# Checks split and moved ahead of the experts, filler matmuls behind the attention, output loads merged and placed ahead of the stores

## The chip, the core and the metric

The kernel runs on one core of one Trainium2 chip. The metric is the device time of one execution in microseconds, the median of three. A core has five engines with a queue of instructions each: TensorE (PE) for matrix products, VectorE (DVE), ScalarE (ACT), GpSimd (POOL) and SyncE (SP), which here issues most of the DMA. An engine works through its queue in order; a wait at its head holds up everything behind it. In the profile PEld is TensorE's loading of weights.

## The reference

Two layers over a tensor of 4 images, 128 channels and 64 x 64 positions (4096 tokens for each image), all in float32:

```python
def reference(x, ...):
    # layer 0
    x = x + _L0_conv_ref(_gn(x), ...)
    # layer 1
    t = _to_tokens(x)
    t = t + _L1_attn_ref(_ln_t(t), L1_attn_Wq, L1_attn_Wk, L1_attn_Wv)
    t = t + _L1_ffn_ref(_ln_t(t), L1_ffn_gate_w, L1_ffn_gate_b, L1_ffn_weight1, L1_ffn_weight2)
    return _from_tokens(t, x)
```

Layer 0 is an attention over the positions whose queries, keys and values are 1x1 convolutions with a PReLU. Layer 1 is an attention over the tokens and then a layer of 64 experts. Each expert picks 8 tokens of an image:

```python
    logits = jnp.einsum('bsd,ed->bse', x, gate_w) + gate_b
    probs = jax.nn.softmax(logits, axis=1)
    vals, idx = jax.lax.top_k(probs.transpose(0, 2, 1), K)
    ...
    pooled = jnp.einsum('bked,bke->bed', gathered, topv)
    h = jax.nn.gelu(jnp.einsum('ebd,edh->ebh', h, weight1), approximate=False)
    out = jnp.einsum('ebh,eho->ebo', h, weight2)
    ...
    outputs = outputs.at[jnp.arange(Bn)[:, None], flat_idx].add(weighted)
```

The chosen tokens are pooled with their weights, the pooled row goes through the expert's two matrices (128 to 512 to 128), and the result is added back to the chosen tokens.

## The kernel before

The softmaxes are computed without subtracting a maximum. The kernel therefore keeps the sums and their inverses (`all_sum`, `all_inv` for layer 0, `top_sum`, `top_inv` for layer 1), and `watch` turns them into one count of good partitions. When the count is below 128, a second, general program runs instead; the data at hand never need it.

**Stages.** `stage(b, layer, ...)` runs the attention of one image and layer: eight blocks of 512 queries, for each of them eight groups of four key tiles (`attention`). Each group is products into `ps`, an exponential on ACT, and the products with the values one group later (`products`). Work for other images is dealt out beside the groups. The last stage is `stage(3, 1, ...)`, image 3, layer 1, with `first_weights` beside it, which loads expert weights ahead of time.

**Behind the attention.** After the last stage the kernel finishes the last block of the last image, with nothing beside it. `finish_attn` combines the parts of the result on VectorE (`u`), multiplies by the value matrix on TensorE (`pv`, in two halves, L647), divides by the sum (`xT`, L655), normalizes the rows (`norm_tokens`, whose power runs on GpSimd, L181), transposes them (`x_c` L356 for the residual, `l` L678 for the gate), and forms the gate's logits (`pg`, L710). `last_route` then finds the eight best tokens for each expert among those of the last block and an earlier list: a chain of some twenty small VectorE instructions from `r_top` (L883) to `zl` (L916). Transposes (`pzT`, L923) and products (`pool`, L928 and L932) end in `pooledT`.

**Experts.** 64 experts run in 16 groups of four. Each group has 2 MB of packed weights, which come by two loads of 1 MB on SP into one of nine places (`places_of`); groups 0 to 8 go into the places 0 to 8, group g + 9 into the place that group g has left. Place 8, `late_place`, is 4096 columns wide and lies where the buffers of the routing lay; it can be loaded only when these have been read. The loop is a pipeline: `first_product(g)` (`ph` L1127 and the copy `hp` L1132), `hidden(g - 1)` (transposes `pht` L1137, bias `hT` L1141, Gelu L1145), `second_product(g - 2)` (`po` L1157). `ph`, `pot` and the product of `watch` share two PSUM buffers (`ms_tile`), so a new one waits until the one before the last has been copied out. `po` uses the two larger buffers (`sc_tile`) that the attention's `ps` used.

After group `half_g + 3`, which is 11, the loop does two things outside its own work: `next(scores)` replaces the eight best values in a row of 4096 on VectorE (L768), and `watch` reduces the four tensors, compares them and counts with a product of one column (L1703 to L1721).

**Output.** For each pair of images, `px` (L1217) spreads the experts' results over the tokens, VectorE adds them to the residual in place (L1224), and ACT issues the stores (L1227). The residual `x2` is loaded into places that the experts have left. Its loads stand on SP behind the weights and behind `first_pair`, the routing weights of images 0 and 1.

**What sets the order.** Instructions are recorded in the order of the program, and a scheduler then orders them for each engine; `keep_in_program_order` fixes an instruction against its neighbours, and `no_sync_barrier` keeps instructions on their side of it. DMAs take one of eight semaphores in turn, from SP and ACT alike, in the scheduled order; a DMA waits until the last user of its semaphore has landed.

Of the kernel before, what the change touches and what calls it, by code (L numbers as in the profile page):

```python
# [9 lines left out]
F32 = mybir.dt.float32  # L10
AF = mybir.ActivationFunctionType
ALU = mybir.AluOpType
AX = mybir.AxisListType
# [13 lines left out]
def tile_unshifted(  # L27
# [58 lines left out]

    x2 = [dram_tile([P, S], f"x2_{b}") for b in range(B)]
    x2_block = [[dram_tile([P, BLK], f"xb_{b}_{n}") for n in range(NB)] for b in range(B)]  # L90

    t1 = [[dram_tile([P, BLK], f"t1_{b}_{n}") for n in range(NB)] for b in range(B)]
# [522 lines left out]
    def finish_attn(b, n):  # L615
# [27 lines left out]
        for k, (s0, ns) in enumerate(((2, 2), (0, 2)) if final else ((0, 3), (3, 1))):  # L643
            pv = ms_tile(f"pv{nm}_{k}")[:, : ns * (C + 1)].rearrange("p (s c) -> p s c", c=C + 1)
            for s in range(ns):
                for h in range(2):
                    nc.tensor.matmul(  # L647
                        pv[bass.ts(h, HC), s, :],
                        lhsT=u[:, (s0 + s) * P + h * HC : (s0 + s) * P + (h + 1) * HC], rhs=wvd,
                        start=True, stop=True,  # L650
                    )
            i = slice((b * NB + n) * SUB + s0, (b * NB + n) * SUB + s0 + ns)
            nc.vector.reciprocal(top_inv[:, i], pv[:, :, C])
            for s in range(ns):
                nc.vector.scalar_tensor_tensor(  # L655
                    xT[:, s0 + s, :], in0=pv[:, s, :C],
                    scalar=top_inv[:, i.start + s : i.start + s + 1], in1=xq[:, s0 + s, :],
                    op0=ALU.mult, op1=ALU.add,
                )
            nc.vector.tensor_copy(top_sum[:, i], pv[:, :, C])  # L660
        yield
        tb = pools["blk"].tile([P, SUB, C], F32, tag="tb", name=f"tb{nm}")
        tg = block_tile("c1", f"tg{nm}")
        if direct:
            norm_tokens(xT, tb, f"l2_{b}_{n}")
            if not final:
                store_tokens(b, n, tb)
            xp = block_tile("xp", f"xp{nm}")
            to_channels(xT, xp, f"x2_{b}_{n}")
            nc.scalar.dma_start(out=x2[b][:, bass.ts(n, BLK)], in_=xp)  # L670
            yield
            if final:

                last_tokens.append(tb)
                for h, copy in enumerate((nc.scalar.copy, nc.vector.tensor_copy)):
                    pt = ms_tile(f"l2_{b}_{n}_{h}")[:, :HB]
                    for s in range(SUB // 2):
                        nc.tensor.transpose(  # L678
                            pt[:, bass.ts(s, P)], tb[:, h * SUB // 2 + s, :], ident
                        )  # L680
                    copy(tg[:, bass.ts(h, HB)], pt)
            else:
                to_channels(tb, tg, f"l2_{b}_{n}")
        else:
            turn_to_channels(
                xT.rearrange("p s c -> p (s c)"), block_tile("xp", f"xt{nm}"),
                x2_block[b][n],
            )
            yield
            norm_tokens(xT, tb, f"l2_{b}_{n}")  # L690
            store_tokens(b, n, tb)
            turn_to_channels(
                tb.rearrange("p s c -> p (s c)"), block_tile("c0", f"tt{nm}"), t2[b][n]
            )
            yield
            yield
            nc.sync.dma_start(out=tg, in_=t2[b][n])
            nc.sync.dma_start(out=x2[b][:, bass.ts(n, BLK)], in_=x2_block[b][n])
            yield
# [264 lines left out]
            yield  # L964


    def run(gen):
        for _ in gen:
            pass
# [74 lines left out]

    def first_weights():

        w1b = block_tile("xq", "w1b", 4)[:E, :]
        nc.sync.dma_start(out=w1b, in_=a["weight1"][:, D1 - 1, :])
        yield from idle(2)
        new_place(6, seq, "k")  # L1050
        new_place(2, extra, "w")
        for g in (6, 2):
            for h in range(2):
                load(g, g, h)
        yield from idle(2)
        pw = ms_tile("pw")
        for c in range(NHC):
            nc.tensor.transpose(
                pw[:, bass.ts(c, E)], w1b.rearrange("e (p c) -> e c p", c=NHC)[:, c, :],
                ident[:E, :E],  # L1060
            )
        nc.scalar.copy(w1bT.rearrange("p c e -> p (c e)"), pw[:, : NHC * E])
        yield from idle(2)
        new_place(7, seq, "v")
        for h in range(2):
            load(7, 7, h)
        yield

    def last_weights(n, g):
# [4 lines left out]
        if n == NB - 1:  # L1074
# [17 lines left out]
    stage(3, 1, chain(done_after(route(2)), first_weights()), None,  # L1092
          ahead=mix_values(3), pace=(2, 1), hook=last_weights)
    products()


    ends["att"].close()
# [7 lines left out]
    for g in range(3, 6):  # L1105
        new_place(g, ring, "w")
        for h in range(2):
            load(g, g, h)
    last_top = last_route(B - 1, pooledT)
    ends["blk"].close()  # L1110
    late = ctx.enter_context(tc.tile_pool(name="late", bufs=1, side="right", reuse_waits="tile"))
    late_place = late.tile([P, S], F32, tag="z", name="late_place")
    place(8, late_place)
    scores = last_scores(B - 1, *last_top)

    for h in range(2):
        load(8, 8, h)
# [58 lines left out]
    for g in range(E // EG + 2):  # L1176
        if g < E // EG:
            first_product(g)
        if 0 <= g - 1 < E // EG:
            hidden(g - 1)  # L1180
        if 0 <= g - 2:
            second_product(g - 2)

        for half, now in ((0, g), (1, g - 2)):
            if 0 <= now and now + 9 < E // EG:
                load(now + 9, now, half)
        if g == half_g + 3:
            next(scores)
            watch(ms_tile("watch")[0:1, 0:1])
    next(scores)  # L1190


# [5 lines left out]
    for i in range(B // 2):  # L1198
        for q in range(2):
            ys.append(places_of[2 * i + q])  # L1200
            for h in range(2):
                tc.keep_in_program_order(
                    nc.sync.dma_start(out=ys[-1][:, h, :], in_=x2[2 * i + h][:, bass.ts(q, HS)])
                )
    for i in range(B // 2):
        pe = ms_tile(f"poe{i}")
        nc.tensor.transpose(
# [471 lines left out]
@with_exitstack  # L1679
def tile_conv_attn_hybrid(ctx: ExitStack, tc: tile.TileContext, a: dict, out: bass.AP):  # L1680

    nc = tc.nc
    guard = ctx.enter_context(tc.tile_pool(name="guard", bufs=1))
    all_sum = guard.tile([P, BLK], F32, tag="all_sum", name="all_sum")
    all_inv = guard.tile([P, P], F32, tag="all_inv", name="all_inv")  # L1690
    nc.gpsimd.memset(all_sum, 0.0)
    nc.gpsimd.memset(all_inv, 0.0)
    top_sum = guard.tile([P, P], F32, tag="top_sum", name="top_sum")
    top_inv = guard.tile([P, P], F32, tag="top_inv", name="top_inv")
    nc.gpsimd.memset(top_sum, 0.0)
    nc.gpsimd.memset(top_inv, 0.0)
    count = guard.tile([1, 1], mybir.dt.int32, tag="count", name="count")

    def watch(pc):
        ok = guard.tile([P, 4], F32, tag="ok", name="ok")  # L1700

        later = tc.keep_in_program_order
        later(nc.vector.tensor_reduce(ok[:, 0:1], all_sum, axis=AX.X, op=ALU.max))  # L1703
        later(nc.vector.tensor_reduce(ok[:, 1:2], all_inv, axis=AX.X, op=ALU.max))
        nc.vector.tensor_scalar(ok[:, 0:1], ok[:, 0:1], SAFE_SUM, None, op0=ALU.is_le)
        nc.vector.tensor_scalar(ok[:, 1:2], ok[:, 1:2], SAFE_INV, None, op0=ALU.is_le)
        later(nc.vector.tensor_reduce(ok[:, 2:3], top_sum, axis=AX.X, op=ALU.max))
        later(nc.vector.tensor_reduce(ok[:, 3:4], top_inv, axis=AX.X, op=ALU.max))
        nc.vector.tensor_mul(ok[:, 2:3], ok[:, 2:3], ok[:, 3:4])
        nc.vector.tensor_scalar(ok[:, 2:3], ok[:, 2:3], SAFE_RATIO, None, op0=ALU.is_le)  # L1710

        later(nc.vector.tensor_reduce(ok[:, 3:4], top_inv, axis=AX.X, op=ALU.add))
        nc.vector.tensor_scalar(ok[:, 3:4], ok[:, 3:4], SAFE_INV, None, op0=ALU.is_le)
        both = guard.tile([P, 1], F32, tag="both", name="both")
        nc.vector.tensor_mul(both, ok[:, 0:1], ok[:, 1:2])
        nc.vector.tensor_mul(both, both, ok[:, 2:3])
        nc.vector.tensor_mul(both, both, ok[:, 3:4])
        ones = guard.tile([P, 1], F32, tag="ones_g", name="ones_g")
        nc.gpsimd.memset(ones, 1.0)
        nc.tensor.matmul(pc, lhsT=both, rhs=ones, start=True, stop=True)  # L1720
        nc.vector.tensor_copy(count, pc)  # L1721

    tile_unshifted(tc, a, out, all_sum, all_inv, top_sum, top_inv, watch)
    good = nc.values_load(count[0:1, 0:1], min_val=0, max_val=P)
    with tc.If(good < P):
        tile_general(tc, a, out)
# [40 lines left out]
```

## Time and profile before

| | us |
|---|---|
| median of three runs | 3296.14 (3294.93 to 3297.43) |
| the profiled execution | 3298.76 |
| its span, first to last instruction | 3297.0 |
| TensorE busy in the span | 3227.0 (98%) |
| VectorE busy | 2123.0 (64%) |
| end of the last attention product | 3179.2 |
| first product of the experts | 3202.5 |
| last product of the experts ends | 3257.2 |
| first add of the output | 3264.4 |
| last add of the output ends | 3286.8 |

The times on the lower half of the table are positions in the span. A row of the profile's timeline gives the start, the duration, the engine, the line, the operation, the tiles written and read, and how many instructions were merged; a float32 product appears as two records. The chain of waits gives start, duration and the instruction that was last on the way to the end. In the table by windows the columns are the length of the window, the busy time of each engine with its number of instructions, the granted clock of TensorE as a share of full speed, the share of the 16 DMA engines that was busy, and the bytes moved in GB/s. A wait line names the waiting instruction, what it waited for, the time in total, the number of waits and the longest.

### The profile page before, as it was taken

Reading aid. Unit: us, or ns where it says so; the run is one execution under the profiler, and the core shown is the slowest. Engines: PE = TensorE matmul, PEld = TensorE weight load, DVE = VectorE, ACT = ScalarE, POOL = GpSimd, SP = SyncE. Lnnn points to the kernel's source line nnn. Section 1 sums busy time; section 2 is a strip of 40 time slices with the busy share of each in tenths; the row PEclk is TensorE's granted clock in tenths of the full one; section 3 lists DMA queues with packets and bytes.
Section 4 is the critical chain, followed back from the end, with each engine's and each line's share of the span. In section 5 each row is a group of like instructions: output and inputs, shape, how many; then the busy total and the mean of one; then the engine's idle time right before and its main releaser. Section 6 shows DMA issues by size and latency. Waiting matters only on the chain.

```text
span 3297.0 us, 49453 instructions
## 1 busy us (share of the span) xinstructions
PE 3227.0 (98%) x19764; PEld 1602.7 (49%) x19764; DVE 2123.0 (64%) x4192; ACT 1253.4 (38%) x1432; POOL 424.4 (13%) x414
## 2 busy tenths in 40 slices
PE   8999999999999999999999999999999999999986
PEld 4444444445555644444555554444444455454443
DVE  6665567556665667756675657765776566666566
ACT  2333334433333335333433335333333333343432
POOL 0111112310000004241000002242100002010011
PEclk9999999999999999999999999999999999999988
DMA  3221244223323222311120111321231010131059
GB/s 88 52 53 28 56 113 122 74 82 80 90 73 85 55 55 54 70 31 36 39 53 23 39 26 39 91 64 26 45 75 39 20 40 20 33 108 39 17 203 373
DMA packets 364753, 223.31 MB, mean 68 GB/s; under 512 B 273632, under 2 KB 298720, under 8 KB 359136
## 3 DMA queue, kind: packets, MB, share of 16 engines
q1 hardware_dynamic: 359056, 208.54, 23.6%
q10 hardware_dynamic: 4944, 10.46, 0.8%
q8 instruction: 157, 2.57, 0.3%
q0 software_dynamic: 512, 1.05, 0.1%
q14 instruction: 84, 0.69, 0.1%
HBM read 159.75 MB, written 97.19 MB: 78 GB/s over the span
## 4 chain that ended last, share of the span: by engine, by line
PE 96%; DVE 2%; DMA 1%; issue 0%; POOL 0%; ACT 0%; SPq 0%; ACTq 0%; DVEq 0%; POOLq 0%
PE ps L542 40%; PE av L476 27%; PE av L504 23%; PE pe L272 1%; PE pa L291 1%; PE pq L445 1%; PE pv L647 1%; PE ph L1127 1%; PE pg L710 0%; PE po L1157 0%; PE pd L590 0%; PE pht L1137 0%; DMA w<-x 0%; DVE tt L490 0%; DMA first_x<-in_x_dram 0%
## 5 line engine op out<-in xcount | busy, mean ns | idle before, releaser
L551 ACT ACTIVATE pt<-ps 128x1024 f32<-128x1024 f32 x1024 | 1021.7, 1024 | 1520.0 <-PE ps L542 1452.7
L542 PE MATMUL ps<-q,t 128*64 128x512 f32 x4096 | 929.3, 593 | 0.0
L476 PE MATMUL av<-pt,asm 64*128 64x512 f32 x4096 | 922.2, 589 | 0.9 <-ACT sw L630 0.9
L566 DVE TENSOR_TENSOR sacc<-sacc,pt 128x1024 f32<-128x1024 f32 x448 | 586.0, 1308 | 290.6 <-ACT pt L551 265.8
L504 PE MATMUL av<-pt,tt 128*64 128x256 f32 x3072 | 637.6, 379 | 0.0
L476 PEld LDWEIGHTS av<-pt,asm 64*128 64x128 f32 x4096 | 395.8, 187 | 485.5 <-issue 470.1
L490 DVE TENSOR_TENSOR tt<-pt 128x512 f32<-128x512 f32 x512 | 356.7, 697 | 372.6 <-ACT pt L551 355.9
L542 PEld LDWEIGHTS ps<-q,t 128*64 128x64 f32 x4096 | 315.8, 137 | 469.4 <-issue 442.1
L504 PE MATMUL av<-tt,mixed 128*64 128x256 f32 x2048 | 526.9, 380 | 5.4 <-DVE tt L490 5.4
L542 PE MATMUL ps<-e,e 64*128 64x512 f32 x2048 | 491.5, 597 | 2.1 <-DMA e<-ye 2.1
L504 PEld LDWEIGHTS av<-pt,tt 128*64 128x64 f32 x3072 | 359.9, 137 | 261.8 <-issue 137.9
L504 PE MATMUL av<-pt,mixed 128*64 128x256 f32 x1024 | 305.5, 380 | 0.0
L504 PE MATMUL av<-tt,tt 128*64 128x256 f32 x1024 | 305.2, 380 | 0.0
L542 PEld LDWEIGHTS ps<-e,e 64*128 64x128 f32 x2048 | 193.0, 187 | 230.5 <-issue 226.6
L504 PEld LDWEIGHTS av<-tt,mixed 128*64 128x64 f32 x2048 | 280.8, 137 | 8.6 <-DVE tt L490 6.3
L181 POOL TENSOR_TENSOR l_y<-l_v,mhalf 128x4 f32<-128x4 f32 x64 | 64.9, 1014 | 1586.8 <-DVE l_v L180 1586.5
L492 DVE TENSOR_TENSOR tt<-pt 128x256 f32<-128x256 f32 x512 | 220.5, 431 | 16.5
L491 DVE TENSOR_TENSOR pt<-tt,pt 128x256 f32<-128x256 f32 x512 | 218.6, 427 | 16.2
L504 PEld LDWEIGHTS av<-pt,mixed 128*64 128x64 f32 x1024 | 140.3, 137 | 61.3 <-DVE pt L491 0.3
L504 PEld LDWEIGHTS av<-tt,tt 128*64 128x64 f32 x1024 | 140.5, 137 | 1.9 <-DVE tt L492 0.7
L585 POOL TENSOR_TENSOR all_sum<-all_sum,c 128x512 f32<-128x512 f32 x32 | 44.0, 1375 | 522.2 <-DVE c L584 522.2
L182 DVE TENSOR_TENSOR l_z<-l_y 128x4 f32<-128x4 f32 x64 | 11.7, 183 | 97.0 <-POOL l_y L181 97.0
(248 smaller groups left out, 1779.3 us busy)
## 6 DMA issues: line engine op xcount, KB each, us to landing
wp<-in_weight_dram SPq DMA_DIRECT2D x128, 256.0 KB
w<-wp SPq DMA_DIRECT2D x22, 1024.0 KB
xq<-in_x_dram SPq DMA_DIRECT2D x32, 256.0 KB
rb<-inv SPq DMA_DIRECT2D x32, 256.0 KB
xT<-xt SPq DMA_DIRECT2D x128, 64.0 KB
ak<-xT SPq DMA_DIRECT2D x32, 256.0 KB
t<-kt SPq DMA_DIRECT2D x128, 64.0 KB
t<-t SPq DMA_DIRECT2D x32, 256.0 KB
```

The costliest lines, as they stand in the source:

```text
L181: nc.gpsimd.tensor_tensor(y[:, :k], v[:, :k], mhalf[:, :k], op=ALU.pow)
L272: nc.tensor.matmul(pe[part, :], lhsT=w12[:, part], rhs=xn, start=True, stop=True)
L291: nc.tensor.matmul(pa[part, bass.ts(s, P)], lhsT=xn[:, bass.ts(s, P)][:, part], rhs=wa, start=True, stop=True,)
L476: nc.tensor.matmul(avs[b, 0, n][:, r, :], lhsT=values[b, 0][rows, j, :], rhs=pt[rows, h, :], start=(j == 0), stop=(j == NJ - 1),)
L490: nc.vector.tensor_sub(tt[:, 0:2, :], p4[:, :, 1, :], p4[:, 0, :, :])
L491: nc.vector.tensor_add(p4[:, 0, 1, :], tt[:, 1, :], p4[:, 0, 0, :])
L492: nc.vector.tensor_sub(tt[:, 2, :], p4[:, 1, 0, :], p4[:, 0, 1, :])
L504: nc.tensor.matmul(av[bass.ts(half, HC), bank, slot, :], lhsT=lhsT, rhs=rhs, start=first, stop=final, skip_group_check=True,)
L542: nc.tensor.matmul(ps[part, h, :], lhsT=key[:, part], rhs=q[rows, :], start=True, stop=True,)
L551: nc.scalar.activation(pt, ps, AF.Exp, scale=scale)
L566: nc.vector.tensor_add(sums[b, n], sums[b, n], pt)
L585: nc.gpsimd.tensor_add(all_sum, all_sum, c1)
```

## The change

Three things are changed.

1. `watch` is split. The part for layer 0 (five VectorE instructions) runs at the start of `first_weights`, in the last stage. The part for layer 1 (eight VectorE instructions) stands behind `last_route`, ahead of the experts. In the loop only the counting product and its copy are left, and these and `next(scores)` come after group `half_g + 2`, which is 10.
2. `keep_busy` puts products of the identity with itself, which nothing reads, into TensorE's queue: 11 behind the last attention product, 2 and 3 behind the two halves of `pv`, 9 behind the transposes `x_c`, and 24 ahead of the transposes `pzT`. They write to an `sc_tile`.
3. `x2` is kept by pairs of images, so that one DMA of 2 MB loads half the columns of both; four loads take the place of eight. A barrier for the scheduler stands between these loads and the output's products, adds and stores.

```diff
-    x2 = [dram_tile([P, S], f"x2_{b}") for b in range(B)]
+    x2_pair = [dram_tile([2, P, S], f"x2_{i}") for i in range(B // 2)]
+    x2 = [x2_pair[b // 2][b % 2] for b in range(B)]
...
             nc.vector.tensor_copy(top_sum[:, i], pv[:, :, C])
+            if final:
+                keep_busy(FILL[1 + k], f"busy_b{k}")
...
             nc.scalar.dma_start(out=x2[b][:, bass.ts(n, BLK)], in_=xp)
+            if final:
+                keep_busy(FILL[3], "busy_c")
...
+    FILL = (11, 2, 3, 9, 24)
+
+    def keep_busy(k, name):
+
+        t = sc_tile(name)
+        for i in range(k):
+            tc.keep_in_program_order(
+                nc.tensor.matmul(t[:, i % 2, :P], lhsT=ident, rhs=ident, start=True, stop=True)
+            )
...
     def first_weights():
 
+        watch(0)
...
     products()
+    keep_busy(FILL[0], "busy_a")
...
+    keep_busy(FILL[4], "busy_d")
     last_top = last_route(B - 1, pooledT)
...
     scores = last_scores(B - 1, *last_top)
+    watch(1)
...
-        if g == half_g + 3:
+        if g == half_g + 2:
             next(scores)
-            watch(ms_tile("watch")[0:1, 0:1])
+            watch(1, ms_tile("watch")[0:1, 0:1])
...
             ys.append(places_of[2 * i + q])
-            for h in range(2):
-                tc.keep_in_program_order(
-                    nc.sync.dma_start(out=ys[-1][:, h, :], in_=x2[2 * i + h][:, bass.ts(q, HS)])
+            tc.keep_in_program_order(
+                nc.sync.dma_start(
+                    out=ys[-1],
+                    in_=x2_pair[i].rearrange("h c t -> c h t")[:, :, bass.ts(q, HS)],
                 )
+            )
+
+    tc.no_sync_barrier()
```

The new `watch` in full; the old one did all of it in one call, with the result of each part multiplied into `both`:

```python
    def watch(layer, pc=None):
        later = tc.keep_in_program_order
        if layer == 0:
            later(nc.vector.tensor_reduce(ok[:, 0:1], all_sum, axis=AX.X, op=ALU.max))
            nc.vector.tensor_reduce(ok[:, 1:2], all_inv, axis=AX.X, op=ALU.max)
            nc.vector.tensor_scalar(ok[:, 0:1], ok[:, 0:1], SAFE_SUM, None, op0=ALU.is_le)
            nc.vector.tensor_scalar(ok[:, 1:2], ok[:, 1:2], SAFE_INV, None, op0=ALU.is_le)
            nc.vector.tensor_mul(ok[:, 0:1], ok[:, 0:1], ok[:, 1:2])
            return
        if pc is not None:
            ones = guard.tile([P, 1], F32, tag="ones_g", name="ones_g")
            nc.gpsimd.memset(ones, 1.0)
            nc.tensor.matmul(pc, lhsT=ok[:, 0:1], rhs=ones, start=True, stop=True)
            nc.vector.tensor_copy(count, pc)
            return
        later(nc.vector.tensor_reduce(ok[:, 2:3], top_sum, axis=AX.X, op=ALU.max))
        later(nc.vector.tensor_reduce(ok[:, 3:4], top_inv, axis=AX.X, op=ALU.max))
        later(nc.vector.tensor_reduce(ok[:, 1:2], top_inv, axis=AX.X, op=ALU.add))
        nc.vector.tensor_mul(ok[:, 2:3], ok[:, 2:3], ok[:, 3:4])
        nc.vector.tensor_scalar(ok[:, 2:3], ok[:, 2:3], SAFE_RATIO, None, op0=ALU.is_le)
        nc.vector.tensor_scalar(ok[:, 1:2], ok[:, 1:2], SAFE_INV, None, op0=ALU.is_le)
        nc.vector.tensor_mul(ok[:, 0:1], ok[:, 0:1], ok[:, 2:3])
        nc.vector.tensor_mul(ok[:, 0:1], ok[:, 0:1], ok[:, 1:2])
```

## The prediction

> **What bounds the kernel now.** I read the page's share by engine, then the stages by windows, then the chain of waits from 3170 us on, then TensorE's and SP's order of work there, and last DMA in stretches. Up to 3179 us the answer is one line: TensorE is busy (29.2 of 30 us in 3150 to 3180), and no instruction of the change stands in that part but five small VectorE ones. After 3179 us it is not:
>
> ```profile
> 3150.00:3180.00 30.00, 29.16 (x208) 14.66 (x204) 17.65 (x33) 15.69 (x27) 5.50 (x6) 1.00 0.26 84
> 3180.00:3202.00 22.00, 9.08 (x42) 6.18 (x42) 13.57 (x53) 5.38 (x11) 2.41 (x3) 0.54 0.94 365
> 3202.00:3236.00 34.00, 33.60 (x505) 19.73 (x504) 19.46 (x29) 6.93 (x11) 0.00 (x0) 0.95 1.00 402
> 3236.00:3242.00 6.00, 0.24 (x10) 0.08 (x2) 5.71 (x15) 0.63 (x1) 0.00 (x0) 0.82 1.01 416
> 3242.00:3262.00 20.00, 15.25 (x220) 8.67 (x220) 9.07 (x15) 8.41 (x10) 2.30 (x1) 0.84 1.01 422
> 3262.00:3287.00 25.00, 20.34 (x64) 5.61 (x64) 21.37 (x18) 3.78 (x4) 7.02 (x4) 0.84 0.89 330
> 3287.00:3297.00 10.00, 0.00 (x0) 0.00 (x0) 0.00 (x0) 0.00 (x0) 0.00 (x0) 0.50 0.65 261
> ```
>
> The last three columns are granted clock, DMA share and GB/s. Between the attention and the experts the clock falls to half; in the experts both TensorE and DMA are full; at 3236 TensorE stands still for 6 us beside a busy VectorE; at the end DMA alone runs. The chain names the stops:
>
> ```profile
> 3202.53 3.49 PE ph L1127 x16
> 3234.42 4.42 DVE late_place L768
> 3241.95 0.19 PE watch L1720 x2
> 3242.14 3.58 PE ph L1127 x16
> 3267.72 4.18 DMA out_dram<-t
> 3271.97 9.32 DMA w<-x
> ```
>
> The last two lines are the load that stands behind a store (SP's waits put 13.8 us to that one store). How full DMA is decides what all this is worth, so I cut it by stretches:
>
> ```profile
> 3198.50:3204.50 6.00, 5.02 (x26) 3.40 (x30) 0.97 (x3) 1.66 (x2) 0.00 (x0) 0.50 0.79 261
> 3210.00:3264.00 54.00, 43.30 (x690) 26.85 (x684) 32.56 (x53) 17.31 (x23) 4.30 (x2) 0.90 1.01 419
> 3264.50:3268.00 3.50, 3.50 (x12) 0.81 (x8) 2.74 (x3) 1.28 (x2) 3.50 (x2) 0.62 0.23 87
> 3273.00:3278.00 5.00, 4.59 (x20) 1.20 (x16) 4.75 (x5) 0.00 (x0) 0.00 (x0) 1.00 0.95 249
> 3278.00:3292.50 14.50, 5.56 (x20) 1.20 (x16) 6.58 (x6) 0.00 (x0) 0.00 (x0) 0.72 1.03 417
> ```
>
> DMA is saturated at 419 GB/s for 54 us and again at 417; only the other three stretches fall short. **So the bound of the last 100 us is DMA, and the change is worth what it fills of DMA's gaps**, not what it takes from TensorE.
>
> **What the Trainium skill says.** "TensorE: Matmul & The Clock Gate", Part 1 (The HAM clock gate): the clock is halved after an idle window of about 3.4 us, restored after a busy one, the window is free-running. The trace agrees: drops at 3181.85, 3239.93 and 3260.35 us and rises at 3205.74, 3246.7 and 3267.2 lie on one grid of 3.41 us; a window busy by about half (21.1 to 24.5 us) was still followed by a drop. "DMA: Bandwidth & Descriptors", Issuing engines are not separate DMA queues: loads of SP and stores of ACT share the same engines. The trace agrees (stores with loads or alone, 3278 to 3292.5, move 417 GB/s, loads alone 419), so an earlier load takes room from a store, and only idle room is a gain.
>
> **The change part by part**, against the profiled execution (span 3297.0, 3298.76 in all; 2.6 us above the median of 3296.14, so I subtract the difference from the median).
>
> *Fills.* 49 matmuls of the identity, 128x128. Nearest row: the convolution's 128x128 products (L291), eight records in 1.05 us at full clock, each 0.273, so (1.05-0.273)/7 = 0.111 apiece and 0.22 a fill of two records; at half clock (1.92 us for eight) 0.44. Batches: 11 take 2.4 in a gap of 3.05 us (before the first pv); 2 take 0.4 in 0.72; 3 take 0.7 in 0.80; 9 take 2.0 in 2.62; 24 take 5.3 in 6.10. Every batch fits if the clock holds. Behind them wait pv, the transposes and the products of the routing, all on the path. What it saves: pv twice 1.13 against about 0.6 (sixteen records take 1.05 elsewhere), on the path about 0.85 with the VectorE work that follows; transposes l about 0.25, since they follow tb; pg 1.65 to about 1.1, 0.5; pool 2.40 to 1.3; pzT 0.2. So ph starts 2.9 us earlier, near 3199.6, and its first sixteen records take 1.7 instead of 3.49. Windows between the batches are 45 to 70% busy by my count, so a drop for one window is likely in some runs; the 24 then end about 1 us late and still leave a fast clock.
>
> *Second half of the checks before the experts.* Eight VectorE instructions ahead of the first hp copy: three reductions 0.2 apart, five of 0.15 with waits: 1.6 us. They cover ph's 1.2 us and delay hp by 0.4. Bounds 0 (ph cold again) and 1.6; I take 0.4. *First half* in the last attention: five instructions, about 1.2 us of VectorE, which has 40% free there: 0.
>
> *What is left at 3236.* The replacement (4.42) stays, but follows hp of group 10, which ended at 3232.5, and no longer hp and hT of 11. The checks after it (3238.87 to 3241.81) are gone, and the watch product waits for nothing. TensorE has 2.5 us of work beside the replacement; then ph of group 12 waits, since its buffer is freed by the count copy behind the replacement. On before's own scale it goes on at 3232.5 + 4.75 = 3237.25 instead of 3241.95: 4.7 gained, with a stall of about 3 us instead of 5.76. From there I walked the built order, with VectorE as the pace of hp, hT and the products: 14.9 us to the last po at full clock, 16.5 if the stall costs the clock; before it is 15.3. I take -0.5. Sum for TensorE: 2.9 (start of ph) + 1.8 (ph's clock) + 0.3 (rest of the ramp) - 0.4 + 4.7 - 0.5 = 8.8 us of gain, 7.5 to 10. The first add goes from 3264.38 to about 3255.6, the first store from 3267.7 to about 3258.5.
>
> *Loads for the output.* Eight of 1 MB become four of 2 MB, all ahead of the stores in SP's order; none waits for a store's semaphore. Their places are free after po of groups 9 to 12, by about 3242. SP's issues fall from eight of 0.32 to four: nothing, as SP waits anyway. The merged load gives up that the first half is there early; both halves were awaited by the same add: 0.
>
> *DMA's sum.* late_place waits for the routing's last reads of its space; it goes from 3199.37 to about 3197.9, before the earlier loads run out (3199.0). From there 16 MB of weights, 2 of first_pair, 8 of x2 and 8 of stores remain, 34 MB or 35.65e6 bytes: 85.1 us at 419. Weights are always asked for in time: the next load needs only ph of group 0, 3200.8, while late_place fills DMA until 3204. All loads end near 3264.5; stores begin near 3258.5, so the gap at 3264.5 is closed with 6 us in hand. Against 3199.3 + 85.1 = 3284.4 I put 1.1 for the change from loads to loads with stores (half of what 3273 to 3278 lost: 5 x (1 - 249/419) = 2.0), and 3.5 to 3.7 from the last data (3293.3) to the end of the span: 3289.1. From the other side, the gaps lost 2.3 (3198.5), about 1.1 (3204.5 to 3210), 2.8 (3264.5) and 2.0 (3273), 8.2 in sum; if 0.5 of them stays, 7.7. **I take -7.8: 3288.3 us.** Both ways lean on one fact, that DMA never waits. VectorE's adds (16 x 1.22 from 3255.6) end by 3278 even when the last load lands at 3272 behind stores, 7 us ahead of DMA's end: what is late next is DMA itself. Bounds: no transition loss, 3287.0; 3 us of it and a late late_place, 3291.
>
> **Rivals.**
> 1. The clock falls anyway and the fills run at 0.44: 9 end 1.4 late, 24 take 7.8 to 10.7, so pzT is 3 to 6 us late, and with it zT and the load of late_place that waits for it. DMA starts its last 34 MB at about 3204.5: the end is 3204.5 + 85.1 + 1.5 + 3.7 = 3294.8, or 3293.9 by the median. For it: half-busy windows lost the clock at 24.5 us. Against: 24 in a row are two windows of full work.
> 2. Slower: loads and stores together run below the full rate. With my times 2.5 MB of loads are left when stores begin; shared evenly that is 5.0 MB of mixture, 11.9 us at 419. In 3273 to 3278 a load ran beside stores at 249: for the whole mixture 20.1, +8.2, which is 3296.5, no change. At 190 or below it is 26.3 us, 3302.7: slower by more than 0.2% from there on. Against: from 3278 to 3281.3 the same load ran beside stores and DMA moved over 400.
> 3. The change does not do what it says, the order of loads and stores being left: excluded by the built order, where the four loads wait for TensorE and earlier loads alone.
>
> **How the numbers follow.** A measurement of this kernel tells 0.2%, 6.6 us, from no change. Forecast 0.67 (own range 3285.6 to 3290.6, one tenth of it above 3289.5), rival 1 0.14, rival 2 mild (no change) 0.08, rival 2 in full or something unseen that costs 0.07, the rest better than the forecast 0.04. Faster 0.60 + 0.04 + a little of rival 1 = 0.68; same 0.07 + 0.13 + 0.05 = 0.25; slower 0.07. The range of 3285.6 to 3293.6 leaves out the second rival and the worst of the first.
>
> **What would show it.** Right: clock 1.0 through most of 3180 to 3202; ph's first records at 0.59 us, near 3199.6; no watch wait of 5.8; DMA over 400 GB/s from 3199 to the end; the last adds waiting for a load, not for TensorE. Wrong: pzT behind busy_d; DMA below 350 while loads and stores mix; a gap in DMA before stores begin.

## The result and the profile after

| | before | after |
|---|---|---|
| median, us | 3296.9 | 3289.84 |
| profiled execution, us | 3298.76 | 3290.02 |
| its span | 3297.0 | 3288.3 |
| end of the last attention product | 3179.2 | 3177.4 |
| from there to the end of the span ("tail") | 117.8 | 110.9 |
| request of late_place's weights after the attention's end | 20.2 | 18.7 |
| first add after the attention's end | 85.2 | 78.7 |

The ratio after to before is 0.9978, with a 95% interval of 0.9971 to 0.9985: faster by 7.06 us, where 7.8 was forecast. One of the sixteen executions behind the median of after took 3427 us at a granted clock of 0.946, a slow run, and is left out of the ratio. The two profiled executions differ by 8.7, of which 1.8 lie before the attention's end and 6.9 in the tail.

The 1.8 us are not the change's. They arise in the first 40 us. The table by windows of the kernel before, then of the changed kernel (columns as in the prediction; the granted clock is third from the right):

```profile
21.80:25.20 3.40, 2.39 (x8) 1.15 (x8) 1.07 (x3) 1.32 (x2) 0.00 (x0) 0.90 0.30 61
25.20:28.60 3.40, 3.40 (x8) 1.50 (x7) 3.25 (x6) 1.84 (x3) 0.00 (x0) 0.50 0.26 51
28.60:32.00 3.40, 3.40 (x14) 2.06 (x15) 2.57 (x5) 0.52 (x2) 0.00 (x0) 0.60 0.13 26
```

```profile
21.80:25.20 3.40, 2.29 (x8) 1.15 (x8) 0.97 (x2) 1.22 (x2) 0.00 (x0) 1.00 0.34 71
25.20:28.60 3.40, 2.64 (x12) 1.64 (x12) 3.40 (x7) 2.09 (x3) 0.00 (x0) 1.00 0.23 44
28.60:32.00 3.40, 3.40 (x17) 2.62 (x17) 2.50 (x5) 1.94 (x2) 0.00 (x0) 1.00 0.16 33
```

The same code lost the clock in one execution and not in the other. From 40 us on the same instructions stand 1.8 us apart, and again at the attention's end (between them one window more was lost by each, near 800 us after and near 920 us before). The Trainium skill, "TensorE: Matmul & The Clock Gate", Part 1, says that the window is free-running and that the number of cold products varies from run to run; these two runs agree. In twelve of the fourteen profiles shown here the attention ends between 3176.7 and 3177.4, in one at 3175.3, and in that of before at 3179.2. So the tail is the fairer measure of a profile, and is used below beside the medians.

What answers to the table by windows of before, for the changed kernel:

```profile
3178.00:3200.00 22.00, 19.05 (x154) 14.97 (x153) 15.73 (x64) 5.57 (x12) 2.61 (x3) 1.00 0.99 388
3200.00:3231.00 31.00, 28.63 (x454) 17.49 (x454) 19.93 (x26) 6.30 (x10) 0.00 (x0) 1.00 1.01 420
3231.00:3235.00 4.00, 3.83 (x44) 1.75 (x44) 2.79 (x5) 0.63 (x2) 0.00 (x0) 0.60 1.00 416
3235.00:3258.00 23.00, 16.09 (x228) 9.36 (x222) 12.52 (x16) 12.82 (x14) 6.59 (x3) 0.93 1.01 421
3258.00:3283.00 25.00, 15.21 (x56) 3.97 (x52) 16.89 (x15) 0.00 (x0) 2.74 (x2) 0.91 1.02 414
3283.00:3288.30 5.30, 0.00 (x0) 0.00 (x0) 0.00 (x0) 0.00 (x0) 0.00 (x0) 0.50 0.13 48
```

The last column is what the reader should see: DMA moves 414 to 421 GB/s without a hole from 3200 to 3283, while TensorE in the fourth row is busy for 16 of 23 us and in the fifth for 15 of 25. The clock (0.5 from 3181.9 to 3205.7 before) is 1.00 from 3178 to 3230. The Trainium skill, "DMA: Bandwidth & Descriptors", Specifications, gives 435 GB/s as the fabric's ceiling; 420 is 97% of it. The same table's 358 GB/s for a core's share of memory is exceeded here, with one core at work.

Timeline rows behind the attention in the changed kernel (start, duration, engine, line, tiles, records, idle time before):

```profile
3177.29 2.72 PE L979 MATMUL busy_a<-ident 128*128 128x128 f32 x22
3189.12 5.62 PE L979 MATMUL busy_d<-ident 128*128 128x128 f32 x48
3195.29 0.43 PE L928 MATMUL pzT<-ident,zl 64*128 64x64 f32 x4 [0.55 <-DVE zl L921]
3197.91 1.07 PE L1147 MATMUL ph<-t,pooledT 128*32 128x512 f32 x8 [0.40 <-issue]
3199.09 1.50 DVE L1152 COPY hp<-ph 128x512 f32<-128x512 f32 x2
```

pzT waits 0.55 us for VectorE's zl and not for the fillers, so they fit. The chain of waits near 3227 of the changed kernel:

```profile
3226.52 4.43 DVE late_place L773
3230.97 0.16 DVE count L1740
3231.17 1.93 PE ph L1147 x8
```

The wait of 5.8 us for the checks is gone; the replacement still stops TensorE, for 2.4 us. In this execution the clock then falls to half from 3231.0 to 3234.5. That does not follow every time: in the run with the old loads below, a stall of the same 2.4 us is not followed by a drop. TensorE is busy for 1.13 of the 3.41 us window before the drop here; there the stall lies across two windows, each with 2.0 us or more of work.

### The profile page after: what moved, and what is told of

The parts are those of the page before. It is cut to its first block, busy times and chain, and to the rows that moved or that the text cites. A ratio compares the mean times of both kernels' runs of the same rounds, so it can differ in the third digit from the quotient of the medians.

```text
span 3288.3 us, 49648 instructions
## 1 busy us (share of the span) xinstructions
PE 3229.8 (98%) x19862; PEld 1610.7 (49%) x19862; DVE 2122.2 (65%) x4192; ACT 1253.3 (38%) x1432; POOL 425.9 (13%) x414
## 4 chain that ended last, share of the span: by engine, by line
PE 96%; DVE 2%; DMA 1%; issue 0%; POOL 0%; ACT 0%; SPq 0%; DVEq 0%; ACTq 0%; POOLq 0%
PE ps L543 40%; PE av L477 27%; PE av L505 23%; PE pe L273 1%; PE pa L292 1%; PE pq L446 1%; PE pv L648 1%; DMA tt<-x 1%; PE pg L715 0%; PE ph L1147 0%; PE pd L591 0%; PE po L1177 0%; PE px L1241 0%; PE pht L1157 0%; DVE tt L491 0%
```

## The experiments

All runs were timed against the kernel before on the same chip. The changed kernel was timed with the result alone, so a difference to it compares two sessions; the medians of before in the four sessions lie between 3296.83 and 3297.22. In the table "DMA lost" is the time that DMA was short of 419 GB/s, the sum of (1 - GB/s / 419) over single microseconds of the trace; 3196 to 3212 (3194 to 3210 for e12_no_last_batch, whose attention ends 2 us earlier) is the stretch where late_place is awaited, the other goes from 3258 until shortly before the last data, around the first stores. "Tail" is as above; tail and losses are those of one profiled execution each.

| run | median, us | before of the same runs | 95% interval of the ratio | tail | DMA lost near late_place | near the stores |
|---|---|---|---|---|---|---|
| before | 3296.9 | | | 117.8 | 3.3 | 5.3 |
| after | 3289.84 | 3296.9 | 0.9971 to 0.9985 | 110.9 | 0.3 | 0.2 |
| e1_no_fill | 3291.39 | 3296.83 | 0.9975 to 0.9991 | 113.6 | 3.3 | 0.2 |
| e2_old_loads | 3291.92 | 3296.83 | 0.9979 to 0.9993 | 112.4 | 0.4 | 2.9 |
| e3_old_watch | 3290.45 | 3296.83 | 0.9970 to 0.9990 | 111.9 | 0.4 | 1.6 |
| e4_eight_loads | 3289.20 | 3296.83 | 0.9967 to 0.9985 | 110.6 | 0.3 | 0.2 |
| e5_split_only | 3293.71 | 3297.22 | 0.9983 to 1.0000 | 114.1 | 2.6 | 2.6 |
| e6_loads_only | 3293.21 | 3297.22 | 0.9980 to 0.9994 | 113.4 | 1.7 | 1.9 |
| e7_fills_only | 3293.82 | 3297.22 | 0.9983 to 0.9996 | 116.2 | 0.6 | 5.5 |
| e8_less_load | 3287.88 | 3297.22 | 0.9963 to 0.9984 | 108.8 | 0.3 | 0.9 |
| e9_short_replace | 3290.01 | 3297.0 | 0.9967 to 0.9986 | 110.7 | 0.4 | 0.2 |
| e10_spare | 3289.69 | 3297.0 | 0.9969 to 0.9987 | 110.7 | 1.4 | 0.2 |
| e11_more_load | 3292.07 | 3297.0 | 0.9980 to 0.9993 | 113.3 | 0.4 | 0.2 |
| e12_no_last_batch | 3290.53 | 3297.0 | 0.9976 to 0.9989 | 110.9 | 1.6 | 0.3 |

The intervals are some 4 to 7 us wide, so medians against before hardly tell variants apart that differ by 1 or 2 us. The tails do it better: take what DMA lost from the tail, and the eleven rows that move the same bytes after the attention (all but e8, e10 and e11) leave 108.9 to 110.4 us, whichever engine was sped up or slowed down. The three others leave 107.6 with 1 MB less, 109.1 with half a MB less and 112.7 with 1 MB more. Most of the scatter that is left is one more stretch, from the end of the data (its last, slower bytes counted as if at 419 GB/s) to the end of the span: 3.6 to 4.8 us in the fourteen profiles. With this taken off as well, the eleven rows leave 105.2 to 105.9 us and the three others 103.4, 104.6 and 108.1. This is bookkeeping: it says that the tail is bytes at 419 GB/s, holes in DMA and that last stretch. What opens and closes a hole is shown by the single runs.

### One part taken out of the change

**Without fillers (e1).**

```diff
-    FILL = (11, 2, 3, 9, 24)
+    FILL = (0, 0, 0, 0, 0)
...
```

> The changed kernel (3289.8 us) without the 49 filler products. DMA theory (DMA sets the end, fillers only let the load of late_place start before the earlier loads run out): that load starts near 3199.4 instead of 3196 to 3198, DMA is below 300 GB/s for some 6 us there and loses about 2.3 us; the rest of the trace is full as before. Time 3292 (3291 to 3293). TensorE theory (the end follows TensorE): its 5.0 us of the prediction's fills come back in full, 3294.8. Third: fillers are worth nothing, 3289.8.

Measured: 3291.39, 1.6 above the changed kernel, late_place asked for 20.2 us after the attention as before. Windows of this run:

```profile
3195.00:3197.00 2.00, 0.60 (x4) 0.50 (x4) 1.86 (x5) 0.12 (x1) 0.00 (x0) 0.50 0.92 385
3197.00:3200.00 3.00, 2.45 (x11) 2.21 (x10) 0.08 (x2) 1.66 (x2) 0.00 (x0) 0.50 0.69 169
...
3206.00:3208.00 2.00, 2.00 (x21) 1.02 (x24) 0.95 (x2) 0.22 (x1) 0.00 (x0) 1.00 0.82 213
```

The hole opens where the loads of the places that the attention left have run out and late_place is not yet asked for: 169 GB/s. A second hole, 213 GB/s at 3206 to 3208, comes behind it: the next loads wait for ph of the first groups, which is late and at half clock here (its first eight records take 1.94 us, 1.07 in the changed kernel), so the first of them is issued 5.1 us after late_place's instead of 3.0. The first add comes 82.3 us after the attention, 3.6 later than in the changed kernel, and the tail is 2.7 longer in this execution. DMA accounts for it: it loses 3.3 us near late_place here against 0.3, and runs full elsewhere. The fillers' worth is the two holes. That the end follows DMA and not the adds is shown by e9 below.

**Output loads as before (e2).**

```diff
...
-                nc.sync.dma_start(
-                    out=ys[-1],
-                    in_=x2_pair[i].rearrange("h c t -> c h t")[:, :, bass.ts(q, HS)],
+            for h in range(2):
...
+                    nc.sync.dma_start(out=ys[-1][:, h, :], in_=x2[2 * i + h][:, bass.ts(q, HS)])
...
-    tc.no_sync_barrier()
```

> The changed kernel with the output's loads as before (eight of 1 MB, no barrier between them and the stores). DMA theory: some loads take a semaphore that a store holds, so they start only after the first store landed (about 3262), while the other loads are done at about the same time: DMA falls short before the stores and once more beside them, 2 to 4.8 us lost, 3292 to 3294.6. TensorE theory: the experts are untouched, 3289.8. If the order of loads and stores was no limit once the stores start early, 3289.8 as well, with loads on SP that wait for a store and no gap in DMA.

Measured: 3291.92, 2.1 above the changed kernel. SP's waits, then the windows around the first stores:

```profile
SPq L1222 <- DMA out_dram<-t: 12.1, 1, 12.1
```

```profile
3262.00:3264.00 2.00, 1.80 (x10) 0.49 (x8) 1.97 (x3) 0.00 (x0) 0.00 (x0) 1.00 0.67 272
3264.00:3270.00 6.00, 5.55 (x22) 1.41 (x20) 5.81 (x6) 0.00 (x0) 0.00 (x0) 1.00 1.01 291
```

A load waits 12.1 us for a store again, and DMA runs at 272 and 291 GB/s for 8 us. Its share in the second row is 1.01 all the same: in this stretch busy DMA engines are not full DMA engines, and only the rate tells. In the second row the last load of 1 MB, which had stood behind the store, moves beside stores (0.93 and 0.82 MB in 6 us); why the two do not fill DMA was not tried.

**Checks in one piece after group 11 (e3).** The replacement goes back behind group 11 with them, and `watch` is that of before.

```diff
-        watch(0)
...
-    watch(1)
...
-        if g == half_g + 2:
+        if g == half_g + 3:
             next(scores)
-            watch(1, ms_tile("watch")[0:1, 0:1])
+            watch(ms_tile("watch")[0:1, 0:1])
...
```

> The changed kernel with the checks in one piece after group 11, as before; fillers and loads of the change stay. TensorE theory: the stall at the checks is 4.7 us longer and the end 4.7 later, 3294.5. Pure DMA theory: no byte moves, 3289.8. DMA theory with the chain of adds: the last store of the changed kernel could have ended near 3280.6 (issued by 3278.05, 1 MB at 419 GB/s), 2.8 before DMA's end at 3283.4; 4.7 late minus 2.8 is 1.9, so 3291.7, with first add near 3261 and full DMA up to the last megabytes.

Measured: 3290.45, 0.6 above, tail 1.0 longer. The first add comes 83.4 us after the attention, 4.7 later than in the changed kernel, and only about a fifth of that reaches the end of the tail. The TensorE theory (3294.5) falls here, and the chain of adds was overrated too (3291.7 expected). What is lost is 1.6 us of DMA from 3262 on, where the loads are done and the stores have just begun.

**Eight loads, barrier kept (e4).** The edit of the second run, with the barrier left in place.

> The changed kernel with eight loads of 1 MB for the output in place of four of 2 MB, but with the barrier that keeps them ahead of the stores. DMA theory: order is all, size nothing: 3289.8 within 0.7, DMA full from 3198 to 3283. Rival: the merging itself counts (fewer semaphores taken, fewer issues on SP), 2 us or more slower, 3292 or above, with loads that wait for one another.

Measured: 3289.20, tail 110.6. No worth of the merging is seen; e2, which differs from this run by the barrier alone, is 2.7 us slower, so the order is what counts.

### One part put into the kernel before

The edits are the split of the checks alone (e5), the loads with the barrier alone (e6), and the fillers alone (e7).

> The kernel before (3296.9 us) with the checks split and moved as in the change; no fillers, loads as before. DMA theory: the gap of DMA at 3199 to 3204 stays (2.3 us), stores start 4.7 us earlier, so the gap at 3264 shrinks to what the run with the old loads showed (about 2.1 us lost in all near the first stores). From the changed kernel that is 3289.8 + 1.6 + 2.1 = 3293.5, 3.4 below before. TensorE theory: 4.7 below, 3292.2. If the checks were worth only what leaving the split out of the changed kernel cost (0.6): 3296.3.

> The kernel before with the merged loads and the barrier alone. DMA theory: the gap at 3199 stays; loads run on to about 3264.5 with none behind a store, the first store comes at 3267.7 as before, so DMA stands for 3 us there, and then runs full: 3289.8 + 1.6 + 3.2 = 3294.6, 2.3 below before. TensorE theory: TensorE is where it was, 3296.9. If order of loads alone were what the change is worth: 3290.

> The kernel before with the fillers alone. DMA theory: late_place is asked for 1.6 us earlier and the gap at 3199 closes; stores start near 3263 instead of 3267.7, loads wait for stores as before, with a gap near 3263 to 3270 like that of the run with the old loads: 3289.8 + 2.1 + 0.6 = 3292.5, 4.4 below before. TensorE theory: 5.0 below, 3291.9. If the fillers were worth only what leaving them out of the changed kernel cost (1.6): 3295.3.

Measured: 3293.71, 3293.21 and 3293.82, that is 3.5, 4.0 and 3.4 below before (the expectations were 3.4, 2.3 and 4.4; the first one's interval ends at 1.0000). Alone the parts bring 10.9 in sum, together 7.1; taken out one by one they cost 1.6, 2.1 and 0.6, 4.3 in sum. They seem to share a gain, though each sum carries the noise of three medians. The trace of the fillers alone shows how, in windows and in SP's waits:

```profile
3196.00:3199.00 3.00, 2.57 (x18) 1.65 (x22) 0.26 (x1) 1.27 (x1) 0.00 (x0) 0.78 1.01 355
...
3260.00:3264.00 4.00, 3.63 (x12) 0.87 (x8) 3.56 (x4) 1.98 (x2) 4.00 (x3) 0.68 0.24 97
```

```profile
SPq L1220 <- DMA out_dram<-t: 14.1, 1, 14.1
```

The hole near late_place is nearly closed, the loads are done earlier, and one of them still stands behind the first store, which comes at 3262.95: DMA idles at 97 GB/s for 4 us. In this execution much of what the fillers won was given back there (tail 116.2, DMA lost 5.5 near the stores, as before). With the loads alone the hole at the stores shrinks to this:

```profile
3263.00:3265.00 2.00, 2.00 (x8) 0.30 (x4) 1.67 (x2) 0.00 (x0) 2.00 (x2) 0.78 0.52 193
```

Near the stores before lost 5.3 us; the split alone leaves 2.6, the order of loads alone 1.9, both together (e1) 0.2, and the fillers alone 5.5. So this hole is closed by starting the stores sooner or by having more to load until they start, and the two share it: 2.7 and 3.4 alone, 5.1 together.

Part of what the loads alone won in their profile is luck. They ask for late_place 19.3 us after the attention's end, 0.9 sooner than before, without a filler: in that execution the clock fell 5.5 us after the attention's end, and 2.7 us after it in the profile of before. Where the clock's windows lie differs from execution to execution, as in the first 40 us above, and here it was worth more than half of the 1.5 us that the fillers gain.

### Bytes against engine time

**One load less (e8), one load more (e11).** The first leaves out the second half of group 12's weights, so that 1 MB less moves; the second adds a load that nothing reads.

```diff
-            if 0 <= now and now + 9 < E // EG:
+            if 0 <= now and now + 9 < E // EG and (now, half) != (3, 1):
```

```diff
+    tc.keep_in_program_order(nc.sync.dma_start(out=places_of[4][:, 0, :], in_=packed[0][:, 0, :]))
     tc.no_sync_barrier()
```

> The changed kernel without one load of 1 MB of expert weights (the second half of group 12, which then uses that of group 3). All waits of TensorE and VectorE stay. DMA theory: 1.05 MB at 419 GB/s is 2.5 us, and the chain of adds has at least that in hand: 3287.3 (3286.8 to 3287.9), every load and store after it 2.5 us earlier. TensorE or VectorE theory: 3289.8 within 0.5.

> The changed kernel with one more load of 1 MB, which nothing reads, into place 4 behind the last load for the output and ahead of the stores. No engine but SP issues anything more and nobody waits for it. DMA theory: 1.05 MB at 419 GB/s more, 2.5 us slower: 3292.3 (3291.8 to 3292.8), DMA full up to the end. TensorE or VectorE theory: 3289.8 within 0.5.

Measured: 3287.88, 2.0 faster, and 3292.07, 2.2 slower, where 2.5 each were expected; the tails are 2.1 shorter and 2.4 longer. The executions of the two do not overlap: eight with less lie from 3287.18 to 3289.52, 21 with more from 3290.52 to 3294.96. The first gave back 0.7 us in a hole at 3262, since its loads end 2.5 us sooner and its stores do not start sooner. The end of the second, then of the changed kernel:

```profile
3274.00:3282.00 8.00, 2.15 (x8) 0.49 (x8) 3.32 (x3) 0.00 (x0) 0.00 (x0) 0.94 1.02 416
3282.00:3287.00 5.00, 0.00 (x0) 0.00 (x0) 0.00 (x0) 0.00 (x0) 0.00 (x0) 0.50 0.73 290
```

```profile
3274.00:3282.00 8.00, 0.73 (x4) 0.00 (x0) 2.03 (x2) 0.00 (x0) 0.00 (x0) 0.78 1.02 415
3282.00:3287.00 5.00, 0.00 (x0) 0.00 (x0) 0.00 (x0) 0.00 (x0) 0.00 (x0) 0.50 0.32 125
```

**TensorE's stall cut (e9).** The replacement runs on 512 of 4096 columns; the rest is left out.

```diff
-        tc.keep_in_program_order(replace(b, top, z))
+            nc.vector.match_replace(
+                out=z[:, : S // 8], in_to_replace=top[half_of(b), :],
+                in_values=M[b // 2][half_of(b), : S // 8], imm_value=-3.0e38,
+            )
```

> The changed kernel with the replacement of the eight best values done on an eighth of its row only (512 of 4096 columns; the rest of that row, and what image 3 adds with it, is left out). It shortens the stall of TensorE near 3227 by some 3.8 us and moves no byte. TensorE theory: 3.8 us faster, 3286.0. DMA theory: the first add and first store come up to 3.8 us earlier, the stores only share DMA with loads sooner, the end stays: 3289.8 within 0.7, DMA full from 3198 to 3283.

Measured: 3290.01, no change. The first add comes at 3252.96 instead of 3256.08, the first store 2.6 us sooner, and the windows of this run read as in the changed kernel:

```profile
3199.00:3260.00 61.00, 53.52 (x743) 30.36 (x736) 35.90 (x51) 19.76 (x25) 9.31 (x4) 0.94 1.01 420
3260.00:3264.00 4.00, 3.61 (x16) 0.90 (x12) 3.90 (x4) 0.00 (x0) 0.00 (x0) 1.00 1.02 420
3264.00:3274.00 10.00, 7.14 (x26) 1.81 (x24) 8.84 (x8) 0.00 (x0) 0.00 (x0) 1.00 1.02 416
```

**Without the last 24 fillers (e12).**

```diff
-    FILL = (11, 2, 3, 9, 24)
+    FILL = (11, 2, 3, 9, 0)
...
```

> The changed kernel without the last 24 filler products (those beside the search for the eight best on VectorE); the other 25 stay. The clock falls during that search, so the first products of the experts are cold and end about 1.6 us later, but the load of late_place waits for the routing's transposes alone, which come at most 0.3 later. DMA theory: 3289.8 within 0.7. TensorE theory: 1.8 to 2.3 us slower, 3291.6 to 3292.1.

Measured: 3290.53, 0.7 above, at the edge of what was expected. The tail is 110.9 as with them, late_place is asked for 18.70 us after the attention (18.69 with them), and the first add comes 3.2 us later. The equal tail does not mean that these fillers buy nothing. Without them the first eight records of ph take 1.93 us instead of 1.07, the loads behind late_place wait up to 4.3 us for ph (2.1 with the fillers), and DMA has a hole there, where the changed kernel moves 410 and 426 GB/s:

```profile
3203.00:3204.00 1.00, 1.00 (x6) 0.57 (x6) 0.31 (x1) 0.00 (x0) 0.00 (x0) 1.00 1.31 311
3204.00:3205.00 1.00, 1.00 (x16) 0.40 (x18) 0.69 (x1) 0.17 (x1) 0.00 (x0) 1.00 0.60 238
```

The data end 107.3 us after the attention's end, 106.1 in the changed kernel. The tails agree only because the last stretch, from the end of the data to the end of the span, is 3.6 us in this execution, the fastest of its 21, and 4.8 in that of the changed kernel. So the last batch is worth about 1 us of DMA, and the median, 0.7 slower, goes the same way. The DMA theory missed it by counting the request of late_place alone.

**An attempt to beat the change (e10).** A quarter of place 5 is moved into memory that is free during the last attention, so that 0.5 MB is loaded there.

```diff
...
+        w5.append(extra.tile([P, EG * H // 2], F32, tag="w5", name="w5a"))
...
+        load5(5, 0)
...
-    for g in range(3, 6):
-        new_place(g, ring, "w")
+    for g in range(3, 5):
+        place(g, ring.tile([P, 2 * EG * H], F32, tag="w", name=f"w{g}", bufs=2))
...
+    w5.append(ring.tile([P, EG * H // 2], F32, tag="w5b", name="w5b", bufs=1))
+    w5.append(ring.tile([P, EG * H], F32, tag="w5c", name="w5c", bufs=1))
...
```

> The changed kernel with a quarter of place 5 (4 KB of each partition, 0.5 MB) taken from the ring into memory that is free during the last attention, so that 0.5 MB of weights is loaded there, where DMA is mostly idle, and 0.5 MB less is left after it. All else as in the change. DMA theory: 0.52 MB at 419 GB/s is 1.25 us, less a few tenths where loads now end before the stores run full: 3288.6 to 3289.0. TensorE theory: nothing, 3289.8. It would be the fastest of all if DMA theory holds.

Measured: 3289.69, nothing. Windows of this run, then of the changed kernel:

```profile
3194.00:3196.00 2.00, 1.06 (x10) 0.76 (x8) 1.71 (x4) 0.35 (x1) 0.00 (x0) 1.00 0.96 401
3196.00:3198.00 2.00, 1.52 (x14) 1.38 (x18) 0.56 (x4) 1.30 (x2) 0.00 (x0) 1.00 0.54 135
```

```profile
3194.00:3196.00 2.00, 1.17 (x11) 0.87 (x9) 1.78 (x5) 0.26 (x2) 0.00 (x0) 1.00 0.99 418
3196.00:3198.00 2.00, 1.42 (x14) 1.31 (x18) 0.45 (x3) 1.41 (x2) 0.00 (x0) 1.00 1.04 356
```

The 1.25 us that the bytes are worth came back as a hole of 1.1 us more in front of late_place, which is asked for at 3195.94 whatever the other loads do. The expectation forgot that the earlier loads now run out sooner. So bytes moved away count only if they lie behind late_place's request, as in e8; ahead of it the routing's chain on VectorE is the bound.

## Why the prediction was right

**The bound: right.** The sum of bytes over rate, from the request of late_place, was the answer. late_place: forecast 1.5 us sooner, measured 1.5 (20.2 to 18.7 after the attention). From the load's start to the last data: forecast 85.1 and 1.1, measured 85.6 (near 3197.9 to 3283.5). The cost of a cold ph for the loads behind late_place stands in the prediction only as the gap of 1.1 at 3204.5 to 3210; it says that weights are always asked for in time, and without the last fillers they were not.

**Fills: right in effect, small in size.** 48 records took 5.62, against 5.3; 22 took 2.72, against 2.4; the short batches 0.71 and 0.94, against 0.4 and 0.7, since the first record's latency of 0.27 was left out of each. ph started 20.6 us after the attention's end (23.4 before), 2.8 sooner against 2.9. The clock held in the profile of the changed kernel; in three of the nine profiles with all fillers (e2, e3, e7) it dropped for one window near 3197, as the prediction thought likely in some runs. Of the prediction's 1.8 us for ph at full clock about 1 reaches the end of the data, through the loads that wait for ph (e12). Rival 1, a clock that falls for the fillers and delays late_place, did not come: late_place is asked for 18.7 us after the attention in the profiles of all ten kernels that have the first four batches.

**Checks before the experts: right.** Eight instructions, 1.3 us against 1.6; hp began 0.1 us after ph's first half was done, against 0.4.

**At 3236: gain right, what follows mis-sized.** From hp of group 10 to the point where TensorE goes on with ph it took 10.4 us with the old checks (3226.72 to 3237.08 in e3) and 5.5 here (3225.70 to 3231.17): 4.9 gained, against 4.7. That the first add of e3 is 4.7 late is another sum: these 4.9, and 1.6 for a window of lost clock near 3197 in e3's profile, minus 1.7, because e3 is faster from the resume on. From the resume (3231.17) to the last po it took 17.75 us; the term was 14.9, 16.5 with the clock lost. The clock was lost (0.60 in 3231 to 3235), and TensorE then stood behind VectorE's copies at full clock too:

```profile
3237.67 0.75 PE L1157 MATMUL pht<-ident,hp 128*128 128x128 f32 x4 [0.82 <-DVE hp L1152]
```

Three waits of 0.8 for hp came after the slow window (one before the change), and in e2, which kept its clock there, the same stretch took 16.8. So both bounds of the walk were too low. TensorE's sum was therefore 6.5 at the first add instead of 8.8 (7.5 to 10), outside its range. It cost nothing: e9 moved the first add by 3 us without moving the end.

**Output loads: right.** No load waits for a store, and the hole before the stores is gone. Mixing loads and stores was priced at 1.1 us in the sum; DMA lost 0.2 in all there (417 GB/s at 3260 to 3264). But little was mixed: the first store is issued at 3258.45, its bytes move only from 3262 on, and by 3265 the loads are done, where the prediction reckoned with a mixture of 5 MB. The better test of rival 2 is e9, whose stores start sooner: from 3258 to 3266, 2.0 MB of loads and 1.3 MB of stores move together, at 401 to 428 GB/s in steps of 2 us. That excludes rival 2 where several loads are queued, and SP's waits exclude rival 3. What ran at 249 GB/s before was the stretch beside one load that stood behind a store, and e2 brought it back (291). Why such a pair is slow stays open.

Two readings of the prediction on this point were wrong. Its stretch of stores "with loads or alone" at 417 GB/s, 3278 to 3292.5, held 0.07 MB of loads and 5.93 MB of stores, so it said nothing about a mixture, and neither did 3278 to 3281.3. And the 5.0 MB of rival 2, counted as the other sums count a MB, are 12.5 us at 419, not 11.9.

**The end: mis-sized.** From the end of the data (3283.5, counted as in the experiments) to the end of the span it was 4.8 us, against 3.5 to 3.7. The forecast rested on the one profile of before (3.6 by this count); the fourteen profiles spread from 3.6 (before, e2, e12) to 4.8 (e1 and the changed kernel), in no order of what was changed. The rate ebbs over about 2.5 us in both profiles; what is longer is the time behind the last data, and why was not tried. The 0.9 too much for mixing and the 1.2 too little here nearly cancel, which is luck.

**What would show it.** One sign was wrong: the last adds do not wait for a load. They run through (the eight adds of the second pair take 9.79 us in a row) and are done at 3276.0, 7.4 us before the last data. What is late is the stores' data, as the forecast had it.

The predicted 7.8 against the measured 7.06 is within what the medians can tell. In the profile the tail fell by 6.9; 0.2 less time to the last data than forecast and 1.2 more behind it make up the difference of 1.0.

## What to carry to other kernels

When a stage moves bytes at a rate that does not change with what the engines do, price each part of a change by the hole in the DMA rate that it closes, and look which holes two parts share: here three parts worth 3 to 4 us each were worth 7 together. Look for the event after which the last large batch of bytes can be asked for: bytes taken out behind it count almost in full (2.0 of 2.5 us here), bytes ahead of it or a faster engine count only until the next hole opens. Compare profiles from a common event near the change, because two windows of lost clock in the first 40 us (6.8 us at half clock) cost 1.8 us, a quarter of this effect. And do not take two equal times for two equal paths: the tails with and without the last 24 fillers agree, and the data behind them end 1.2 us apart.

## What was not expected of the hardware

- Loads and stores mixed lost next to nothing when several loads were queued: 401 to 428 GB/s from 3258 to 3266 in e9, against 420 for loads alone. The changed kernel shows it for 3 us only.
- With loads queued, a store waits: the first store of the changed kernel is issued at 3258.45 and its bytes move from 3262 on, 3.5 us later; in before, where DMA stands idle, it is issued at 3267.3 and bytes move from 3268 on.
- A DMA share of 1.0 went with 291 GB/s for 6 us (e2, 3264 to 3270), so the share does not show a full DMA.
- The scaling of `oe` (128x128 on VectorE) took 2.39 us beside subtractions on GpSimd, which take 2.34 each (rows of the changed kernel's timeline):

```profile
3253.73 7.01 POOL L954 TENSOR_TENSOR M<-M,late_place 64x1024 f32<-64x1024 f32 x3
3253.77 2.39 DVE L1236 TENSOR_SCALAR oe<-oe,inv_tot 128x128 f32<-128x128 f32 x1
```

It starts 0.04 us after a subtraction and ends within 0.1 us of that one's end. The same instruction took 1.36 us where it started 1.08 us into the subtraction before, and in e9 0.75 us where it started 1.7 us into one; each time it ended 0.1 us after the subtraction. The Trainium skill, "SBUF — State Buffer", SBUF: two separate sides, says that VectorE in some of its forms and GpSimd take one pair of ports by an exclusive lock for a whole instruction; these rows agree with that, though no run here took GpSimd's work away. It lies on the way to the first add, and by e9 its removal would bring nothing here.
